# Last image of a two-layer kernel on one core: reciprocals spread by TensorE, the next layer's convolution inside the projection, depthwise taps shared with TensorE

## The chip, the cores and the metric

One core of one Trainium2 chip runs the whole kernel. The metric is the device time of one execution in microseconds (us). A core has five engines that run beside each other and wait for each other through semaphores: TensorE (PE, matrix products; PEld is its loading of weights), VectorE (DVE), ScalarE (ACT), GpSimd (POOL) and SyncE (SP, which here issues DMA transfers). PE writes only to the accumulation memory PSUM (eight banks of 128 partitions by 512 numbers of four bytes); the other data lies in the on-chip memory SBUF.

## The reference, cut to what matters

Eight images of 512 channels and 64 x 64 pixels pass through two layers, each added to its own input. All is in float32.

```python
# layer 0: attention with sampled keys and values
q = einsum('oc,bchw->bohw', w_q, gn(x))           # gn: mean and variance over 16 channels and all pixels
...                                               # 256 sampled positions per image and head -> k, v
attn = softmax(einsum('bhid,bhjd->bhij', q * scale, k))
out = einsum('bhij,bhjd->bhid', attn, v)
x = x + einsum('oc,bchw->bohw', w_out, out) + b_out

# layer 1: bottleneck
y = einsum('bchw,oc->bohw', gn(x), conv_w) + conv_b   # 512 -> 32 channels
z = depthwise_conv(y, dw_w) + dw_b                    # 3x3, stride 2: 64x64 -> 32x32
u = fc2(fc1(z))                                       # over the 1024 pixels, through 256
v = depthwise_deconv(u, de_w) + de_b                  # 3x3, 32x32 -> 64x64
x = x + einsum('bchw,oc->bohw', v, out_w) + out_b     # 32 -> 512 channels
```

## The kernel before, in words

An image lies in SBUF as nine slots of 512 pixels by four chunks of 128 channels; eight of them are pixel tiles, t = 0 to 7. Input, queries and outputs of tile t use different slots of the ring (`x_tile`, `q_tile`, `out_tile`), so that the output of tile t lies where the queries of tile t - 1 were. Two images are held at once (`region`, `spot`).

The order of all work is written out by hand in one loop over g (L1098), one step for each image, tile and pair of heads (256 steps), and LAG = 6 further steps which let the projections of the last tile finish. A step issues `weighted_values` (L591; the products of exponentials and values), in every second step `sum_exps` (L615; the denominators, by products with a selection matrix into the PSUM tile pn), then `logits` of the next step, and `project_out` (L661) for the step six earlier: eight products of 128 x 64 weights with 512 columns into one bank, then on DVE an addition of bias and residual (L674) and the tile's statistics (L677, kept in `st`). Beside this, a generator issues the work of layer 1 for the image before and the queries of the image after; for the last image there is none of the latter.

After the fourth pair of heads of a tile, `invert` (L634) takes the reciprocal of the denominators on DVE (rn, L638), and four small DMAs (L644) copy rows so that each group of 32 partitions has what it needs. `scale_two` (L647) then, two pairs of heads at a time, spreads a row over 32 partitions with a DVE shuffle (L651) and multiplies the attention output with it (L653). `load_residual` (L655) fetches the residual of tile t into its output slot, when the projection of the tile before no longer reads it as queries.

For the last image layer 1 runs alone, after the loop (`layer1_last`, L1157). `layer1` (L730) begins with the loads of the fc2 weights (L736) and `group_stats` (L164): aggregates per chunk on DVE (L169), a product with a 128 x 128 matrix that averages over groups of 16 channels (L173), variance on DVE (L177 to L179), a second such product (L182), and a power of -0.5 on POOL (L185). The convolution weights are scaled by the result (cw, L743). The convolution (py, L750) is 2 halves x 4 chunks x 4 blocks of rows, 32 products of 128 x 32 weights with 512 columns; ACT copies both halves to y (L762); the mean's part comes as 16 products with one column (pb, L768) and is added on DVE (L777). Three copies (L779) bring the last row of one block of rows to the next. The depthwise convolution is nine DVE instructions (L795, L797), each over 256 numbers with a column of weights; then a transpose (pz, L803), fc1 (ph L814, pht L828) and fc2 (pu, L848). `upsample` (L867) makes the transposed convolution of one half of the pixel rows and one parity a of rows, on DVE (L881, L883): three instructions for a = 0 and six for a = 1.

`project_last` (L949) then takes six banks at a time: output products of 32 x 128 weights (L893), and for each result either one addition on DVE (L980), or, for two of the eight tiles, an evacuation on ACT (L977) and an addition on POOL (L978). Each result goes out with its own DMA of 256 KB from SP (L983), 32 in all. Last, a check on the size of the logits (L1163 to L1178) decides on a second path, which these inputs don't take.

Of the kernel before, what the change touches and what calls it, by code (L numbers as in the profile page):

```python
# [49 lines left out]
def kernel(  # L50
# [610 lines left out]
    def project_out(b, t, oc, st):  # L661
# [3 lines left out]
        for hp in range(NCC):  # L665
            for r in (0, DH):
                nc.tensor.matmul(  # L667
                    pp[r : r + DH, :],
                    wout[:, hp, oc * P + r : oc * P + r + DH],
                    ao[:, hp, :],  # L670
                    start=(hp == 0),
                    stop=(hp == NCC - 1),
                )
        nc.vector.scalar_tensor_tensor(  # L674
# [53 lines left out]


    def layer1(b, st, project, place, v):  # L730
# [10 lines left out]
        gs = yield from group_stats(st, 1, b)  # L741
        cw = small.tile([P, NCC, CB], F32, tag="cw", name=f"cw_{b}")
        nc.vector.tensor_mul(cw, convw, gs[:, 1].unsqueeze(2).to_broadcast([P, NCC, CB]))  # L743
        yield None

        py = [ps_mm.tile([P, TP], F32, tag="mm", name=f"py_{b}_{h}") for h in range(2)]
        for h in range(2):
            for cc in range(NCC):
                for rb in range(4):
                    nc.tensor.matmul(  # L750
                        py[h][rb * CB : (rb + 1) * CB, :],
                        cw[:, cc, :],
                        out_tile(b, 2 * rb + h)[:, cc, :],
                        start=(cc == 0),
                        stop=(cc == NCC - 1),
                    )

        y = wflat[:, : (ROWS + 1) * (HW + 1)].rearrange("p (r c) -> p r c", c=HW + 1)
        nc.vector.memset(y[:, :, 0:1], 0.0)
        nc.vector.memset(y[0:CB, 0:1, :], 0.0)  # L760
        for h in range(2):
            nc.scalar.copy(  # L762
                y[:, 1 + 8 * h : 9 + 8 * h, 1:], py[h].rearrange("p (r c) -> p r c", c=HW)
            )
        pb = ps_mm.tile([P, TP], F32, tag="mm", name=f"pb_{b}")
        for cc in range(NCC):
            for rb in range(4):
                nc.tensor.matmul(  # L768
                    pb[rb * CB : (rb + 1) * CB, 0:1],
                    cw[:, cc, :],  # L770
                    gs[:, 0, cc : cc + 1],
                    start=(cc == 0),
                    stop=(cc == NCC - 1),
                )
        yb = small.tile([P, 1], F32, tag="yb", name=f"yb_{b}")
        nc.vector.tensor_sub(yb, col(V_CONVB), pb[:, 0:1])
        nc.vector.tensor_scalar_add(y[:, 1:, 1:], y[:, 1:, 1:], yb)  # L777
# [11 lines left out]
        z3 = z.rearrange("p (i j) -> p i j", j=32)  # L789
        for k in range(9):  # L790
# [3 lines left out]
            if k == 0:  # L794
# [89 lines left out]

        for h, a in ((0, 0), (0, 1), (1, 0)):
            upsample(h, a)
            yield None
# [100 lines left out]
    def layer1_last(b, st, other):  # L988
        return layer1(b, st, project_last(other), spot(other, 0), wbuf[:, 0:2, :])
# [69 lines left out]
    with tc.manual_schedule():  # L1059
# [38 lines left out]
        for g in range(len(names) + LAG):  # L1098
# [12 lines left out]
            summed = g % 2 == 0 and 0 <= g - 1 < len(names)  # L1111
            if g % 2 == 0:
                scale_two()
            if g < len(names):
                weighted_values(*names[g])
            if summed:
                sum_exps(*names[g - 1])
            if g < len(names):
                add_exps(*names[g])
# [24 lines left out]
            if 0 <= k < len(names) and k % NCC < 2:  # L1144
                load_residual(*names[k + k % NCC], 2)
# [11 lines left out]
        drain(layer1_last(B - 1, st1s.pop(B - 1), B - 2))  # L1157
# [118 lines left out]
```

## Time and profile before

The time before is 3290.07 us, the median of three runs (3289.28 to 3290.38).

| what | us |
|---|---|
| median of the runs | 3290.07 |
| the profiled execution | 3290.23 |
| its span, first to last instruction | 3288.5 |
| last loop product of attention values and projection pp(6,1) ends | 3193.1 |
| reciprocal of the last tile ends | 3197.8 |
| projections pp(6,2) and pp(6,3) end | 3201.1 |
| projection of the last tile, pp(7,0) to pp(7,3), ends | 3221.7 |
| convolution py ends | 3237.1 |
| depthwise result z complete | 3243.8 |
| fc2 (pu) ends; its bias added (u) | 3251.1; 3252.07 |
| first addition of an output block on DVE (L980) | 3258.2 |
| last store issued | 3282.4 |

pp(t,oc) is the projection of tile t to output chunk oc. Times from the start of the span are read from the chain of waits and from the timeline of the last 100 us, which list instructions by start and length. In the timeline a product of float32 shows as two records, and records of a column-tiled product overlap, so that the distance between starts, not the length of one, tells the rate. A name such as rn or pp is the program's name for a tile, and L638 is a line of the kernel. The granted clock (PEclk) is given as a share of full speed.

### The profile page before, as it was taken

The numbers are of one execution on the slowest core, as the hardware profiler recorded it, in microseconds if no ns is written. First come the engines' busy times: TensorE is split into PE (matmuls) and PEld (weight loads), VectorE is DVE, ScalarE is ACT, GpSimd is POOL, SyncE is SP. The second block draws the span as 40 slices with busy tenths as digits, with TensorE's granted clock in tenths as the row PEclk, the third lists the DMA queues.
The fourth block names the chain that finished last, engine by engine and source line by source line (L and its number), as shares of the span: only waits on it lengthen the run. The fifth ranks groups of instructions, "written<-read, shape, count | busy, mean of one in ns | idle before, by whom it ended". The sixth has DMA issues, their size and how long they took to land.

```text
span 3288.5 us, 46198 instructions
## 1 busy us (share of the span) xinstructions
PE 3207.7 (98%) x18196; PEld 1531.2 (47%) x18196; DVE 2330.8 (71%) x3786; ACT 1186.2 (36%) x1641; POOL 612.2 (19%) x576
## 2 busy tenths in 40 slices
PE   6999999999999999999999999999999999999996
PEld 5884223348332583326733276332853338433222
DVE  7884765787757777587765977668776687757564
ACT  2343333343333433344333443324433344333520
POOL 1130300130402304022030221303021040310201
PEclk9999999999999999999999999999999999999996
DMA  7232222672327623284333843248232482322713
GB/s 275 77 93 76 76 78 65 198 156 75 113 91 213 126 86 103 78 235 115 104 100 103 209 100 111 83 160 194 71 104 89 181 180 65 121 73 77 130 44 125
DMA packets 293874, 390.62 MB, mean 119 GB/s; under 512 B 18320, under 2 KB 157840, under 8 KB 293648
## 3 DMA queue, kind: packets, MB, share of 16 engines
q1 hardware_dynamic: 240368, 261.72, 24.4%
q0 software_dynamic: 53280, 125.86, 17.1%
q8 instruction: 145, 2.38, 0.3%
q14 instruction: 81, 0.66, 0.1%
HBM read 193.52 MB, written 192.94 MB: 118 GB/s over the span
## 4 chain that ended last, share of the span: by engine, by line
PE 94%; DVE 4%; issue 1%; ACT 0%; DMA 0%; SPq 0%; POOL 0%; ACTq 0%; DVEq 0%; POOLq 0%
PE pp L667 27%; PE pq L275 23%; PE ps L580 14%; PE pa L598 13%; PE pn L625 4%; PE pqt L324 4%; PE pk L533 2%; PE py L750 2%; PE pv L560 2%; PE po L893 2%; DVE rn L638 1%; PE po L424 0%; PE pu L848 0%; DVE st L201 0%; PE po_s L893 0%
## 5 line engine op out<-in xcount | busy, mean ns | idle before, releaser
L667 PE MATMUL pp<-image,wout 128*64 128x512 f32 x3584 | 821.3, 600 | 3.6 <-DVE image L653 3.4
L588 ACT ACTIVATE es<-ps 128x1024 f32<-128x1024 f32 x512 | 504.0, 1022 | 274.0 <-PE ps L580 211.1
L667 PEld LDWEIGHTS pp<-image,wout 128*64 128x64 f32 x3584 | 237.3, 137 | 549.5 <-issue 474.6
L598 PE MATMUL pa<-es,vt 128*64 128x512 f32 x2048 | 488.9, 598 | 1.7 <-ACT es L588 1.7
L275 PE MATMUL pq<-image,wbuf 128*128 128x256 f32 x2048 | 476.3, 381 | 3.3 <-DVE image L217 1.9
L519 POOL DMA_INDIRECT g<-qd,row x256 | 280.4, 1095 | 1056.2 <-DVE row L516 990.0
L580 PE MATMUL ps<-image,kt 64*64 64x512 f32 x3584 | 437.3, 602 | 0.3
L275 PEld LDWEIGHTS pq<-image,wbuf 128*128 128x128 f32 x2048 | 381.8, 191 | 56.0 <-issue 5.0
L674 DVE SCALAR_TENSOR_TENSOR image<-pp,vec,image 128x512 f32<-128x512 f32 x224 | 167.2, 746 | 337.8 <-PE pp L667 334.2
L605 ACT COPY image<-pa 128x512 f32<-128x512 f32 x224 | 131.9, 589 | 658.9 <-PE pa L598 650.5
L610 DVE TENSOR_TENSOR es<-es,es 128x1024 f32<-128x1024 f32 x256 | 310.9, 1215 | 71.4 <-PE pa L598 71.4
L598 PEld LDWEIGHTS pa<-es,vt 128*64 128x64 f32 x2048 | 137.3, 137 | 294.5 <-issue 274.1
L580 PEld LDWEIGHTS ps<-image,kt 64*64 64x64 f32 x3584 | 114.4, 132 | 307.4 <-issue 182.0
L638 DVE RECIPROCAL rn<-pn 128x512 f32<-128x512 f32 x64 | 214.6, 3353 | 7.7 <-PE pn L625 5.8
L334 ACT COPY qr<-pqt 128x512 f32<-128x512 f32 x224 | 131.0, 585 | 238.7 <-PE pqt L324 223.8
L185 POOL TENSOR_TENSOR gs<-ve,nhalf 128x4 f32<-128x4 f32 x16 | 16.6, 1040 | 1022.5 <-DVE ve L184 1022.5
L651 DVE STREAM_SHUFFLE rb<-rn 128x512 f32<-128x512 f32 x256 | 187.4, 732 | 0.1
L275 PE MATMUL pq<-es,es 128*128 128x256 f32 x768 | 181.5, 379 | 0.0
L945 POOL DMA_DIRECT2D out_dram<-part x126 | 138.1, 1324 | 153.9 <-ACT part L940 146.6
L201 DVE BATCH_NORM_STATS2 st<-image 128x6 f32<-128x512 f32 x256 | 159.2, 678 | 7.5 <-DMA image<-in_x_dram 7.4
L677 DVE BATCH_NORM_STATS2 st<-image 128x6 f32<-128x512 f32 x224 | 155.6, 695 | 7.7
L653 DVE TENSOR_TENSOR image<-image,rb 128x512 f32<-128x512 f32 x224 | 155.2, 693 | 7.8
(197 smaller groups left out, 3491.6 us busy)
## 6 DMA issues: line engine op xcount, KB each, us to landing
qd<-qr SPq DMA_DIRECT2D x256, 256.0 KB
image<-in_x_dram SPq DMA_DIRECT2D x112, 512.0 KB
out_dram<-image SPq DMA_DIRECT2D x49, 1024.0 KB
image<-in_x_dram POOLq DMA_DIRECT2D x48, 1024.0 KB
out_dram<-part POOLq DMA_DIRECT2D x126, 256.0 KB
image<-in_x_dram SPq DMA_DIRECT2D x16, 1024.0 KB
wbuf<-in_w_kvT_dram SPq DMA_DIRECT2D x14, 1024.0 KB
out_dram<-spare POOLq DMA_DIRECT2D x56, 256.0 KB
```

The costliest lines, as they stand in the source:

```text
L201: nc.vector.bn_stats(st[:, cc, t, :], x_tile(b, t)[:, cc, :])
L275: nc.tensor.matmul(bank[:, o * 2 * P : (o + 1) * 2 * P], w[:, k, o * P : (o + 1) * P], xh[:, k, :], start=(k == 0), stop=(k == 1),)
L519: nc.gpsimd.indirect_dma_start(held[-1][:, i, :, :].rearrange("p j d -> p (j d)"), None, qd[:, :], bass.IndirectOffsetOnAxis(ap=row[:, ky, ...
L580: nc.tensor.matmul(ps[k : k + DH, a, :], kt[r : r + DH, hp, kc * P + k : kc * P + k + DH], qt[r : r + DH, hp, :], start=True, stop=True,)
L588: nc.scalar.activation(e, ps, AF.Exp)
L598: nc.tensor.matmul(pa[a * DH : (a + 1) * DH, :], vt[:, kc, hd * DH : (hd + 1) * DH], es[kc][:, a, :], start=(kc == 0), stop=(kc == 1),)
L610: nc.vector.tensor_add(es[0], es[0], es[1])
L638: nc.vector.reciprocal(rn, denominators.pop((b, t)))
L651: nc.vector.stream_shuffle(rb, rn, [2 * (hp % 2) + hp // 2] * 32)
L667: nc.tensor.matmul(pp[r : r + DH, :], wout[:, hp, oc * P + r : oc * P + r + DH], ao[:, hp, :], start=(hp == 0), stop=(hp == NCC - 1),)
L674: nc.vector.scalar_tensor_tensor(xt[:, oc, :], pp, col(V_BOUT + oc), xt[:, oc, :], ALU.add, ALU.add)
L677: nc.vector.bn_stats(st[:, oc, t, :], xt[:, oc, :])
```

## The change

Only the end of the last image is touched. The loop now has 256 steps instead of 262, and what its last six did is written out after it:

- The denominators of the last tile are summed, and their reciprocal rn is taken. The four DMAs and the shuffles are gone for this tile. Instead eight products with a column of the identity matrix as broadcast weights spread the rows of rn over 64 partitions each, into four banks, and DVE multiplies the attention output by these, all four pairs of heads, ahead of the projection pp(6,3).
- ACT scales the identity matrix by ten columns of depthwise weights, which gives ten diagonal matrices, in the tiles that held exponentials.
- `last_tile` projects the four chunks of tile 7. After three of the four pairs of heads of chunk oc it issues the statistics of chunk oc - 1 (`mean`) and the scaling of the convolution weights of chunk oc - 2 (`scale`). The convolution follows by chunks, with the statistics of the last chunk among them, and the mean's part ahead of the last two chunks.
- The bias and the mean's part are added when py is copied from PSUM, one half on ACT, one on DVE.
- Taps 5 to 8 of the depthwise convolution are products with diagonal matrices, into a bank that DVE adds to its own sum of taps 0 to 4.
- In the transposed convolution, the odd rows (six taps for each half) are products with diagonal matrices, written to every second column of a bank, and ACT moves them out with the bias. The even rows stay on DVE. All of them are issued ahead of the output products.

Other images take the same instructions as before (`convolve` and `convolve_mean` are only moved out).

```diff
-    def project_out(b, t, oc, st):
+    def project_out(b, t, oc, st, between=None):
...
+            if between:
+                between(hp)
...
+    def last_tile(b, st):
...
+        def mean(cc):
+            c = slice(cc, cc + 1)
+            nc.vector.bn_aggr(mv[:, cc, :], st[:, cc].rearrange("p t s -> p (t s)"))
+            nc.tensor.matmul(gps[0][:, c], group, mv[:, cc, 0:1], start=True, stop=True)
+            nc.vector.tensor_copy(gs[:, 0, c], gps[0][:, c])
+            nc.vector.tensor_sub(dv[:, c], mv[:, cc, 0:1], gs[:, 0, c])
+            nc.vector.tensor_mul(dv[:, c], dv[:, c], dv[:, c])
+            nc.vector.tensor_add(dv[:, c], dv[:, c], mv[:, cc, 1:2])
+
+        def scale(cc):
+            c = slice(cc, cc + 1)
+            nc.tensor.matmul(gps[1][:, c], group, dv[:, c], start=True, stop=True)
+            nc.vector.tensor_scalar_add(ve[:, c], gps[1][:, c], EPS)
+            nc.gpsimd.tensor_tensor(gs[:, 1, c], ve[:, c], nhalf[:, c], ALU.pow)
+            nc.vector.tensor_scalar(cw[:, cc, :], convw[:, cc, :], gs[:, 1, c], None, ALU.mult)
+
+        def between(oc):
+            def step(hp):
+                if hp == 2 and oc >= 1:
+                    mean(oc - 1)
+                    if oc >= 2:
+                        scale(oc - 2)
+
+            return step
+
+        for oc in range(NCC):
+            project_out(b, t, oc, st, between(oc))
...
+        convolve(b, py[:, 0, :], cw, 0, 0)
+        scale(2)
+        convolve(b, py[:, 1, :], cw, 1, 0)
+        convolve(b, py[:, 0, :], cw, 0, 1)
+        mean(3)
+        convolve(b, py[:, 1, :], cw, 1, 1)
+        scale(3)
+        for cc in range(NCC - 1):
+            convolve_mean(pb, cw, gs, cc)
+        for h in range(2):
+            convolve(b, py[:, h, :], cw, h, 2)
+        convolve_mean(pb, cw, gs, 3)
+        for h in range(2):
+            convolve(b, py[:, h, :], cw, h, 3)
+        return (py[:, 0, :], py[:, 1, :]), pb
...
+            py, pb = conv()
+            nc.vector.tensor_sub(yb, col(V_CONVB), pb)
+            for h in range(2):
+                to, fr = y[:, 1 + 8 * h : 9 + 8 * h, 1:], py[h].rearrange("p (r c) -> p r c", c=HW)
+                if h:
+                    nc.vector.tensor_scalar_add(to, fr, yb)
+                else:
+                    nc.scalar.activation(to, fr, AF.Identity, bias=yb)
...
+            if diag and k > 4:
+                nc.tensor.matmul(pd, diag[V_DWW + k], yk, start=(k == 5), stop=(k == 8))
+                if k == 8:
+                    nc.vector.tensor_add(z, z, pd)
...
+            for h, tag in enumerate(("pa", "pn")):
+                upsample(h, 0)
+                pv = ps_a.tile([P, TP], F32, tag=tag, name=f"pv_{b}_{h}")[:, : 2 * P]
+                rows = pv.rearrange("p (r c) -> p r c", c=HW)
...
+                    for n, (k, dr, dc) in enumerate(taps):
+                        nc.tensor.matmul(
+                            rows[:, :, c::2],
+                            diag[V_DEW + k],
+                            u[:, 4 * h + dr : 4 * h + dr + 4, dc : dc + 32],
+                            start=(n == 0),
+                            stop=(n == len(taps) - 1),
+                        )
+                nc.scalar.activation(
+                    v[:, h, :].rearrange("p (r c) -> p r c", c=HW)[:, 1::2, :],
+                    rows,
+                    AF.Identity,
+                    bias=col(V_DEB),
+                )
...
-        for g in range(len(names) + LAG):
+        for g in range(len(names)):
...
-        drain(layer1_last(B - 1, st1s.pop(B - 1), B - 2))
+
+        b, t, st = B - 1, NT - 1, st1s.pop(B - 1)
+        sum_exps(*names[-1])
+        rn = small.tile([P, TP], F32, tag="rn", name="rn_last")
+        nc.vector.reciprocal(rn, denominators.pop((b, t)))
+
+        diag = {}
+        for i, w in enumerate([V_DWW + k for k in range(5, 9)] + [V_DEW + k for k in (0, 1, 2, 6, 7, 8)]):
+            diag[w] = es4[i // 8][:, i // 4 % 2, i % 4 * P : (i % 4 + 1) * P]
+            nc.scalar.activation(diag[w], ident, AF.Copy, scale=col(w))
+        project_out(b, t - 1, 2, st)
+        rb = [ps_s.tile([P, 2, TP], F32, tag="s", name=f"rb_last_{i}") for i in range(2)]
+        for hp in range(NCC):
+            for a in range(2):
+                row = CB * (2 * a + hp % 2) + hp // 2
+                nc.tensor.matmul(
+                    rb[hp // 2][a * DH : (a + 1) * DH, hp % 2, :],
+                    ident[:, row : row + 1].to_broadcast([P, DH]),
+                    rn,
+                    start=True,
+                    stop=True,
+                )
+        for hp in range(NCC):
+            ao = q_tile(b, t)[:, hp, :]
+            nc.vector.tensor_mul(ao, ao, rb[hp // 2][:, hp % 2, :])
+        project_out(b, t - 1, 3, st)
+        for oc in (0, 2):
+            load_residual(b, t, oc, 2)
+        drain(layer1_last(b, st, b - 1, lambda: last_tile(b, st), diag))
```

## The prediction

> **What bounds the kernel now.** The page first: it says that TensorE is the chain that ended last for 94% of the span, so a change of one image's ending can only win the stretch in which PE waits there.
>
> ```profile
> span 3288.5 us, 46198 instructions
> PE   6999999999999999999999999999999999999996
> PEclk9999999999999999999999999999999999999996
> PE 94%; DVE 4%; issue 1%; ACT 0%; DMA 0%; SPq 0%; POOL 0%; ACTq 0%; DVEq 0%; POOLq 0%
> ```
>
> Both PE and its granted clock are full until the last of the 40 slices (82 us each). The second view is the chain of waits in order of time over the last 100 us; columns are start, length, what.
>
> ```profile
> 3194.48 3.34 DVE rn L638
> ...
> 3199.71 1.69 DMA rn<-rn
> ...
> 3207.32 14.39 PE pp L667 x56
> ...
> 3226.52 1.04 POOL gs L185
> ...
> 3227.93 9.18 PE py L750 x64
> ...
> 3248.96 2.18 PE pu L848 x28
> ```
>
> From 3194 the chain leaves PE (reciprocal, a DMA of rows, shuffles and products on DVE), returns for the projection of the last tile (end 3221.7), leaves it for the statistics (six small steps), and then alternates up to the first output product. Third, windows of 1 us and 2 us (length, then busy time of PE, PEld, DVE, ACT, POOL with counts, then clock, DMA share, GB/s):
>
> ```profile
> 3204.00:3205.00 1.00, 0.67 (x4) 0.20 (x4) 1.00 (x2) 0.00 (x0) 0.00 (x0) 0.90 0.88 303
> 3205.00:3206.00 1.00, 1.00 (x4) 0.00 (x0) 0.97 (x4) 0.00 (x0) 0.00 (x0) 0.50 0.94 221
> 3211.00:3212.00 1.00, 1.00 (x4) 0.16 (x4) 0.92 (x2) 0.00 (x0) 0.00 (x0) 0.69 0.29 100
> 3246.00:3247.00 1.00, 1.00 (x12) 0.18 (x4) 0.00 (x0) 0.00 (x0) 0.00 (x0) 0.50 0.00 0
> 3267.00:3269.00 2.00, 2.00 (x9) 0.97 (x9) 1.83 (x6) 0.42 (x2) 1.27 (x1) 0.50 1.03 381
> 3281.00:3283.00 2.00, 0.00 (x0) 0.00 (x0) 0.00 (x0) 0.00 (x0) 0.00 (x0) 0.50 0.72 261
> ```
>
> Each idle stretch costs twice: the wait, and half a clock for the matmuls behind it. And from 3265 the DMA engines are full (381 GB/s) with the 32 stores of 256 KB: the ending is a fixed drain behind the first output block, so what the change wins is how much earlier that block comes. The timeline has the first L980 (output addition on DVE) at 3258.16.
>
> **What the Trainium skill says.** TensorE: Matmul & The Clock Gate, Part 1 (What's actually happening): the clock is halved or restored at the ends of free-running windows of about 3.4 us, by how busy PE was in one. The trace agrees: it falls near 3204.9, rises near 3211.7, falls near 3225.6, rises near 3232.1, falls near 3242.7, that is 2, 4, 2 and 3 such windows apart. A window with PE busy 1.42 of 3.4 us (3201.5 to 3204.9) ended in half clock, one with 1.73 (3235.6 to 3239.0) didn't. The same page (Architectural detail) calls VectorE's queue strict FIFO; the trace has nothing against it. PSUM — Partial Sum Buffer, Specifications (TRN2), says that any non-contiguous access slows matmuls significantly, without a figure; no matmul of the kernel before writes PSUM with a step, so nothing here shows it.
>
> **The change part by part.** Times are on the span of the profiled execution.
>
> *Reciprocals.* Gone: four DMAs of rows, four shuffles, and the wait between projections. The order on PE is now: denominators, pp(6,2), eight spreading products, pp(6,3), tile 7. pp(6,2) ends at 3197.5 as before (32 matmul records of two projections took 7.09 us, 3.55 each); rn is ready at 3197.85. The spread has the shape of a projection (eight products, 128x64 weights, 512 columns): 3.55 us, to 3201.4. DVE meanwhile does pp(6,2)'s addition and statistics (0.68 + 0.69, to 3199.2) and four multiplications; reading PSUM I take L674's 0.75 rather than L653's 0.69, so 3202.3. pp(6,3) hides them (to 3205.0). So tile 7 starts with no wait at 3205.0, against pieces from 3203.15 and mostly from 3207.3 at half clock. The residual loads still wait for pp(6,3), which reads the same buffer: before, they were issued at 3200.3 and the first 512 KB had moved by 3203.2; 2.9 us after 3205.0 is 3207.9, 0.6 us ahead of the first need (3208.55). The fc2 and fc1 loads behind them on SP come 5 us later and are needed at 3236 and after. The ten diagonals are some 3 us on ACT (ten of L822's size or less, 0.3 each), where nothing is until the image's evacuation: nothing.
>
> *Statistics inside the projection.* 4 x 3.55 = 14.2 us, plus five small products in PE's stream. L173's pair of records took 0.36 alone; I take that (bounds 0.12, the weights being prefetched, and 0.5): 1.8. Each waits for DVE, and DVE's queue has the POOL power (1.03) in it, with the weight scaling behind it. Per chunk DVE does copy, sub, mul, add, eps (1.0), waits 1.1, scales (0.2), adds (0.75), statistics (0.69), aggregate (0.3): 4.1, while PE takes 3.55 + 0.72; about level, and I add one stall of 0.2. Projection's end: 3205.0 + 14.2 + 1.8 + 0.2 = 3221.2, against 3221.7: the early start is spent on the insertions.
>
> *Convolution.* A chunk of four products is 8 of 64 records; at full clock the groups of four records took 0.43, so 0.86 a chunk. After 3221.2: two chunks and a small product and a third chunk to +2.95. DVE is late: its queue holds the scaling of chunk 1 (to +1.1), the last addition and statistics (+2.55), then scale(2) with its POOL wait (+4.0), and only then the last aggregate (+4.3). So mean(3) holds PE from +2.95 to +4.35. Then copy to add (+5.5), chunk to +5.55, scale(3) to +5.95, POOL to +7.2, weights at +7.4; PE in the meantime does means and chunks 4 to 6, ending at +8.1, and the last two at +9.8: 3231.0. Before: 3237.1. Gain 6.1.
>
> *Evacuation.* Before, a copy (0.6) and an addition over both halves (0.77): 1.41. Now bias in the evacuation, ACT and DVE each a half; DVE's 512 from PSUM about 0.7 (0.41 for L795's 256, plus 256 columns): +0.75. Gain 0.65. The three row copies (0.6) stay: y at 3232.4, against 3239.15.
>
> *Depthwise.* Before 0.42 + 8 x 0.52 = 4.6. Now DVE 0.42 + 4 x 0.52 = 2.5, with four diagonal products on PE beside it (two L275 records of 0.217 each, 1.75 in all), and an addition from PSUM (0.45): 3.0. Gain 1.6: z at 3235.4, against 3243.8.
>
> *fc1, fc2.* Nothing changed, but before they ran at half clock: pz 0.66, ph 1.97, pht 1.08, pu 2.18, 5.9 of 7.36 us. Now PE's gaps ahead are 1.4 and 1.4 us, not 6.6. If the clock holds, 2.95 less: u at 3235.4 + 4.4 + 0.95 = 3240.8, against 3252.07. Gain 11.3 in all; 8.3 if it doesn't hold.
>
> *Upsampling.* Before, the first output addition began 6.1 us after u, since DVE did all 18 taps. Now DVE does six (2.0), PE twelve. A 128-column product with new weights: L324's records stand 0.117 apart, two a tap: 0.235, 2.8 in all, at full clock. Output products stand behind both halves' taps on PE; + 0.6 for one, 0.05: first addition at u + 3.45. The taps write PSUM at step 2; if that doubles them, u + 6.25. Bounds 1 and 2 times; I take 1.5: u + 4.85, gain 1.25. The evacuation on ACT (0.4) is beside PE.
>
> *Drain.* 30.3 us from the first addition to the end. 8.39 MB at 381 GB/s is 22.0; the first 6 us before moved 232 to 380. With output products at full clock I take 0.5 off (0 to 1.5).
>
> Sum: 11.3 + 1.25 + 0.5 = 13.05, less 0.3 for semaphore hops in the new steps: 12.75. The profiled execution took 3290.23 (span 3288.5), which is 0.16 above the median 3290.07; 3290.23 - 12.75 = 3277.5.
>
> **The rivals.**
> A, as above, the clock full from 3211 on. For it: with the windows where they stand in the trace, the new stages fill them by half or more (pd 1.75 us in one, pz, ph and pht 2.0 in the next). Best, 1-times taps and 1.5 at the drain: 3290.23 - 15.2 = 3275.0; worst, 2-times taps, insertions of 0.5: 3280. Chance 0.62.
> B, the clock falls between the convolution and fc1. Worst window (from pd's end): pz and ph, 1.5 of 3.4 us, between the 1.42 that fell and the 1.73 that didn't, and the window's phase is free. Then fc1 and fc2 give nothing (8.3), taps take 5.6 at half clock and the first addition comes at u + 6.7 (loss 0.6): 8.3 - 0.6 + 0.5 - 0.3 = 7.9, 3282.3; from 3279 (falls late) to 3286. Chance 0.24.
> C, the insertions stall PE: residuals land 2 us later, or a POOL hop is 2 us, and mean() holds the projection in each of three chunks, some 5 us, partly recovered as DVE is then less behind: 3290.23 - 12.75 + 5 = 3282.5, and with a half clock inside 3285. Against it: the margins of 0.2 to 0.6 us above. Chance 0.08, half of it within 0.2%.
> D, slower: one mechanism, the step-2 writes to PSUM in the twelve taps. Each tap would have to be over 1.4 us (6 times 0.235) to eat the gain, and 2 us for 0.2% slower. At 10 times, 28.2 us, the first addition is at u + 28.9: 22.8 later than before, less 11.0 + 0.5: 3301.5. For it: the page's word and no row. Against: half the columns are merely skipped. Chance 0.06.
>
> **How the numbers follow.** A measurement of this kernel can tell about 0.2%, 6.6 us, from no change. Faster: A 0.62, three quarters of B 0.18, a quarter or so of C 0.02: 0.82. Within: the rest of B and C, 0.12. Slower: D, 0.06. The time is A's, 3277.5. The range, 3274 to 3284.5, is A's own with 1 us below it and most of B; left out are D, the bad part of C and the tail of B.
>
> **What would show it.** PE without a gap of over 0.5 us from 3197.9 to the projection's end near 3221; one wait of about 1.4 us behind the last aggregate; py's end near 3231; PEclk full at fc1; the first L980-type addition near 3245.7; 28 to 30 us of stores behind it. Wrong if the clock falls at fc1 (B), if a tap takes over 0.47 us, or if the projection's end is beyond 3224.

## The result, and the profile after

The changed kernel takes 3277.48 us (median of 6 runs, 3276.30 to 3278.57); beside it the kernel before took 3289.68 us (6 runs, 3288.31 to 3290.38). That is 12.2 us less, a ratio of 0.9964 (95% interval 0.9954 to 0.9974). In a later comparison it was 12.1 us less. The forecast was 3277.5. The profiled execution took 3278.57 us, the slowest of the six and 1.1 above the median, with a span of 3276.8.

The forecast total is right to a tenth of a microsecond, but it is not right by its own steps: the clock fell at fc1, which was rival B, and other steps made good for it. That they balance so closely is luck. The rest of this text is about that.

First the lines of the page that answer to those shown of the kernel before:

```profile
span 3276.8 us, 46318 instructions
PE   6999999999999999999999999999999999999997
PEclk9999999999999999999999999999999999999998
PE 94%; DVE 3%; issue 1%; ACT 0%; DMA 0%; SPq 0%; POOL 0%; ACTq 0%; DVEq 0%; POOLq 0%
```

Only the last slice differs: 7 for 6 in PE, 8 for 6 in its clock. At this scale nothing can be read of where the time went, so the chain of waits is next (start, length, what):

```profile
3194.33 3.35 DVE rn_last L1269
3197.72 3.65 PE rb_last L1280 x16
3201.37 9.44 PE pp L667 x44
...
3229.15 0.70 ACT wbuf L833
3229.88 0.77 DVE wbuf L831
...
3235.34 1.59 PE ph L896 x16
...
3238.79 2.18 PE pu L930 x28
...
3241.94 4.88 PE pv L980 x24
...
3247.92 7.40 DVE image L1090 x11
```

From the reciprocal's end to the end of py PE has no gap worth the name: the spread, then 44 records of projections in 9.44 us, which is pp(6,3), pp(7,0) and three quarters of pp(7,1). The chain leaves PE again only with the evacuation. Behind it the two rows to note are pu, 2.18 us as in the chain of the kernel before, and pv, the new taps, 4.88 us. Both are long because of the clock: the windows show its fall, and two experiments below show what full clock gives (columns as before: length, busy time of PE, PEld, DVE, ACT, POOL, then clock, DMA share, GB/s):

```profile
3202.00:3203.00 1.00, 1.00 (x8) 0.36 (x6) 0.71 (x2) 0.00 (x0) 0.00 (x0) 1.00 0.00 0
3233.00:3234.00 1.00, 0.00 (x0) 0.00 (x0) 0.86 (x3) 0.00 (x0) 0.00 (x0) 1.00 0.00 0
3235.00:3236.00 1.00, 0.67 (x12) 0.48 (x16) 0.28 (x1) 0.00 (x0) 0.00 (x0) 0.88 0.00 0
3236.00:3237.00 1.00, 0.90 (x12) 0.02 (x2) 0.00 (x0) 0.05 (x1) 0.00 (x0) 0.50 0.00 0
3246.00:3247.00 1.00, 1.00 (x11) 0.88 (x14) 0.00 (x0) 0.15 (x1) 0.00 (x0) 1.00 0.00 0
```

Where the kernel before had 0.50 at 3205 and 0.69 at 3211, the clock now is 1.00 right through the projection and the convolution. It falls once, near 3235.8 (0.88 over 3235 to 3236 means that it was halved for about the last quarter), and is back near 3246. The hole ahead of the fall is plain: in the microsecond from 3233 PE does nothing, because DVE still has taps of its own when the diagonal products are done.

The same stages side by side; the last two columns are this case's main reading. The forecast lengths are those of the prediction.

| stage | before, ends | after, ends | length after | length forecast |
|---|---|---|---|---|
| reciprocal of tile 7 | 3197.82 | 3197.68 | | |
| spread and pp(6,3); tile 7 starts | 3203.15, mostly 3207.3 | 3204.80 | 7.1 | 7.15 |
| projection of tile 7 | 3221.71 | 3220.38 | 15.6 | 16.2 |
| convolution py | 3237.11 | 3229.13 | 8.75 | 9.8 |
| y complete | 3239.14 | 3231.27 | 2.14 | 1.4 |
| z complete | 3243.8 | 3234.33 | 3.06 | 3.0 |
| u | 3252.07 | 3241.89 | 7.6 | 5.4 |
| first output addition | 3258.16 | 3247.92 | 6.0 | 4.85 |
| end of the span | 3288.5 | 3276.8 | 28.9 | 29.8 |

The gain, read down the two columns of ends, is 1.3 us at the projection's end, 8.0 at py's, 7.9 at y, 9.5 at z, 10.2 at u and at the first addition, and 11.7 at the end. So more than half of it, 6.7 us, comes between the end of the projection and the end of py, where the kernel before waited for the statistics and then convolved.

### The profile page after: what moved, and what is told of

Read it like the earlier page. It is cut to its first block, busy times and chain, and to the rows that moved or that the text cites. A ratio compares the mean times of both kernels' runs of the same rounds, so it can differ in the third digit from the quotient of the medians.

```text
span 3276.8 us, 46318 instructions
## 1 busy us (share of the span) xinstructions
PE 3209.6 (98%) x18256; PEld 1535.1 (47%) x18256; DVE 2325.3 (71%) x3781; ACT 1188.6 (36%) x1652; POOL 614.0 (19%) x579
## 4 chain that ended last, share of the span: by engine, by line
PE 94%; DVE 3%; issue 1%; ACT 0%; DMA 0%; SPq 0%; POOL 0%; ACTq 0%; DVEq 0%; POOLq 0%
PE pp L667 27%; PE pq L275 23%; PE ps L580 14%; PE pa L598 13%; PE pqt L324 4%; PE pn L625 4%; PE pk L533 2%; PE pv L560 2%; PE po L1003 2%; PE py L733 1%; DVE rn L638 1%; DVE image L1090 0%; PE po L424 0%; PE pu L930 0%; DVE st L201 0%
## 5 line engine op out<-in xcount | busy, mean ns | idle before, releaser
L598 PE MATMUL pa<-es,vt 128*64 128x512 f32 x2048 | 489.1, 598 | 1.7 <-ACT es L588 1.7
L598 PEld LDWEIGHTS pa<-es,vt 128*64 128x64 f32 x2048 | 137.4, 137 | 294.7 <-issue 274.8
L185 POOL TENSOR_TENSOR gs<-ve,nhalf 128x4 f32<-128x4 f32 x15 | 15.6, 1042 | 895.6 <-DVE ve L184 895.6
```

The costliest lines, as they stand in the source:

```text
L598: nc.tensor.matmul(pa[a * DH : (a + 1) * DH, :], vt[:, kc, hd * DH : (hd + 1) * DH], es[kc][:, a, :], start=(kc == 0), stop=(kc == 1),)
```

## The experiments

Times of a run are medians, with the kernel before run on the same chip beside them (3288.87 beside the first four, 3290.11 beside the next four, 3289.88 beside the last four). The span's first 3189 us shift by up to 2 us from one execution to the next, so stages are compared by their distance from the end of the last products of exponentials and values (the chain's last pa, L598, at 3189.45 after and 3189.61 before, where the main part ends). Each change below is made to the changed kernel.

**Part by part: the spread alone.** The last tile's spread stays; the projection is not interleaved, and layer 1 is the one of the kernel before.

```diff
-        diag = {}
...
-        drain(layer1_last(b, st, b - 1, lambda: last_tile(b, st), diag))
+        for oc in range(NCC):
+            project_out(b, t, oc, st)
+        drain(layer1_last(b, st, b - 1))
```

> The reciprocals' part alone; statistics, convolution, depthwise steps and upsampling as in the kernel before. Theory (each part is worth what its own stage shows, and the parts add): tile 7 starts without a wait at 3204.7 and, with nothing inserted, its projection ends 14.2 us later at 3218.9, 2.8 us ahead of the kernel before; from there the stages of the kernel before take their 36.5 us to the first output addition and 30.3 us to the end, span 3285.7. Rival (the early start was spent on the insertions alone, and elsewhere a later stage absorbs it): projection ends near 3219 but the span is within 1 us of 3288.5.

Measured: 3285.73 us (12 runs), 3.1 below the kernel before (ratio 0.9992, 0.9983 to 1.0001; the interval takes in no change, so the stages of the trace have to tell). The projection ends 29.12 us after the last pa, against 32.10 before and 30.93 in the changed kernel. Two terms follow. The spread by TensorE with its full clock is worth 3.0 us at the projection's end. And the five small products of the statistics cost the projection 30.93 - 29.12 = 1.8 us. Only 1.37 us of it is their own time; the rest is in their neighbours, as the changed kernel's chain shows:

```profile
3214.71 0.31 PE pa_last L766 x2
3215.03 0.22 PE pn_last L774 x2
3215.25 3.58 PE pp L667 x16
3218.83 0.31 PE pa_last L766 x2
3219.15 0.22 PE pn_last L774 x2
3219.37 1.01 PE pp L667 x4
3220.38 0.99 PE py_last L733 x8
```

No "issue" and no DVE stands between these lines: the statistics were never late. A run of 16 records between two insertions takes 3.58 us, while the 44 uncut ones took 9.44, that is 3.43 per 16.

**Without the spread.** The inverse, the four DMAs and the shuffles come back; all else is as changed.

```diff
-        rn = small.tile([P, TP], F32, tag="rn", name="rn_last")
-        nc.vector.reciprocal(rn, denominators.pop((b, t)))
+        invert(*names[-1])
...
         project_out(b, t - 1, 2, st)
-        rb = [ps_s.tile([P, 2, TP], F32, tag="s", name=f"rb_last_{i}") for i in range(2)]
...
+        scale_two()
         project_out(b, t - 1, 3, st)
...
+        scale_two()
```

> Row DMAs and shuffles as in the kernel before for the last tile; everything behind is that of the changed kernel. Theory: TensorE waits 2 us from 3201 and in pieces to 3207.3, falls to half clock, and the projection ends at 3221.7 plus the 1.4 us of inserted products, 3223.1, 2.7 us later than in the changed kernel; all later stages move with it, span 3279.5. Rival (in the projection with statistics inside it DVE sets the pace, so TensorE's wait is hidden): under 1 us later, span 3277.5 or less.

Measured: 3281.34 us (9 runs), 7.5 below the kernel before (0.9975, 0.9965 to 0.9985), so 4.7 of the changed kernel's 12.2 are lost. The projection ends 34.09 us after the last pa, 3.2 later than with the spread. The chain of this run shows how:

```profile
3194.87 3.34 DVE rn L638
...
3200.10 1.68 DMA rn<-rn
...
3208.51 0.69 DVE image L653
...
3209.26 5.27 PE pp L667 x16
```

From the reciprocal's end (3198.21) to the last multiplication (3209.20) DVE and the DMA hold the chain for 11 us, and the 16 records behind it take 5.27 us for 3.58 because the clock was halved in the gap. The remaining 1.5 us or so of the loss by medians is not settled by this run.

**Without the diagonal products**, depthwise taps and upsampling all on DVE again:

```diff
-        diag = {}
...
-        drain(layer1_last(b, st, b - 1, lambda: last_tile(b, st), diag))
+        drain(layer1_last(b, st, b - 1, lambda: last_tile(b, st)))
```

> Spread and chunked convolution kept, depthwise and transposed convolution all on DVE as before. Theory: y at 3231.3 as in the changed kernel, z 4.6 us later at 3235.9, fc1 and fc2 at half clock (8.3 us to u), first output addition at u + 6.1 = 3250.3, then 30.3 us of drain at half clock: span 3280.6, 3.8 us above the changed kernel. Rival (the diagonals give only the depthwise 1.6 us, and the drain is the stores' alone, 28.9 us): span 3279.2 or less.

Measured: 3280.81 us (10 runs), 8.1 below the kernel before (0.9975, 0.9965 to 0.9984). pz, which waits for z, starts 46.58 us after the last pa, against 44.93: the four depthwise diagonals are worth 1.65 us, as forecast (1.6). fc1 and fc2 ran at half clock here too, from 3232. By the medians all ten diagonals are worth 8.1 to 12.2, 4.1 us; z gives 1.65 of them and the first addition 2.3 in all (60.8 against 58.47). The rest is not settled by this run.

**Upsampling alone on DVE**, the four depthwise diagonals kept:

```diff
-        if diag:
+        if False:
```

> As the changed kernel, but the odd rows of the transposed convolution stay on DVE (depthwise diagonals kept). The taps on TensorE took as long as DVE did before, so the first output addition should come at u + 6.1, as in the changed kernel within 0.3 us (near 3248.0). Theory (the taps' only gain is that they bring TensorE back to full clock ahead of the output products): clock stays 0.50 in the output products, 30.3 us from the first addition to the end, span 3278.3. Rival (the drain is set by the stores and the clock does not matter there): 28.9 us, span 3276.9.

Measured: 3278.64 us (3277.09 to 3280.16, 8 runs), 10.2 below the kernel before (0.9968, 0.9957 to 0.9979): the taps on TensorE are worth about 2 us by the medians, though the ranges of the two kernels overlap. Its profiled execution, the lowest of its runs, is a lesson on its own. There ph took 1.12 us and pht 0.65, and only pu was at half clock (2.18): the same instructions up to u as in the changed kernel, but the clock fell later. So where the clock falls differs from one execution to the next, and a single profile of this kernel carries about 1 us of luck. The fall, at 3236.70, also came behind 3.41 us (from 3233.29) in which the profile has PE busy for 2.05: more than the 1.81 (3235.52 to 3238.93) that kept the clock in the kernel before.

The traces also show what this luck is. Within each trace the falls and rises of the clock are whole multiples of 3.41 us apart: 3235.77, 3246.01 and 3266.49 in the changed kernel (3 and 6 of them), 3204.80, 3211.63, 3225.28, 3232.11 and 3242.35 in the kernel before (2, 4, 2 and 3). But this grid lies elsewhere in the work from one execution to the next. Counted from the last pa, the clock fell after 46.32 us in the changed kernel. Here it was kept at the step after 45.02 us and fell at the next, after 48.43 us.

**One tile or two.** In the changed kernel y's two halves leave PSUM one after the other, not beside each other as forecast. The theory: both halves of py are one PSUM tile, so that the first reader waits for the last product of both, and the second reader for the first. Two tiles:

```diff
-        py = ps_s.tile([P, 2, TP], F32, tag="s", name=f"py_{nm}")
-        pb = ps_s.tile([P, 2, TP], F32, tag="s", name=f"pb_{nm}")[:, 0, 0:1]
+        py = [ps_s.tile([P, 2, TP], F32, tag="s", name=f"py_{nm}_{h}")[:, 0, :] for h in range(2)]
+        pb = ps_mm.tile([P, TP], F32, tag="mm", name=f"pb_{nm}")[:, 0:1]
```

> As the changed kernel, but the two halves of py are two PSUM tiles instead of two banks of one. In the changed kernel ACT's half began only when both halves were done, and DVE's half only when ACT's was done: 1.51 us from py's end. Theory (the waits belong to the shared tile): ACT begins one chunk earlier, DVE at py's end, the evacuation ends 0.8 us after py's end, 0.7 us saved. Rival (the waits belong to the shared destination y, or to the two readers of PSUM): DVE still waits for ACT, 0.1 us or less saved.

Measured: 3276.59 us (5 runs), 13.5 below the kernel before (0.9962, 0.9948 to 0.9977). The two instructions in the timeline of the changed kernel (start, length, engine, line; in brackets the idle time before and who ended it), where py ended at 3229.13:

```profile
3229.15 0.69 ACT L833 ACTIVATE wbuf<-py_last,yb 128x512 f32<-128x512 f32 x1 [36.15 <-PE py_last L733]
...
3229.88 0.75 DVE L831 TENSOR_SCALAR wbuf<-py_last,yb 128x512 f32<-128x512 f32 x1 [2.28 <-ACT wbuf L833]
```

and with two tiles, where py ended at 3228.19:

```profile
3227.35 0.69 ACT L833 ACTIVATE wbuf<-py_last,yb 128x512 f32<-128x512 f32 x1 [35.29 <-PE py_last L733]
...
3228.21 0.75 DVE L831 TENSOR_SCALAR wbuf<-py_last,yb 128x512 f32<-128x512 f32 x1 [1.56 <-PE py_last L733]
```

DVE's releaser changes from ACT to PE, and ACT now runs 0.84 us ahead of py's end, when its own half is done. From py to the start of pz it is 4.59 us for 5.25, 0.66 less. This is shown.

**A filled window.** The theory on fc1 and fc2: the clock is judged by how busy PE was in a window of about 3.4 us (the Trainium skill, TensorE: Matmul & The Clock Gate, What's actually happening; the grid of 3.41 us found above agrees), and the window that ends at the fall, 3232.36 to 3235.77, holds 1.33 us of PE. Three more products of the last depthwise diagonal, into a bank of PSUM that nobody reads, close the hole and change nothing else:

```diff
                 nc.tensor.matmul(pd, diag[V_DWW + k], yk, start=(k == 5), stop=(k == 8))
                 if k == 8:
+                    pf = ps_a.tile([P, TP], F32, tag="pa", name=f"fill_{b}")
+                    for _ in range(3):
+                        nc.tensor.matmul(pf[:, :NK], diag[V_DWW + k], yk, start=True, stop=True)
```

> As the changed kernel, with three more products of the last depthwise diagonal behind the four, into a bank that nobody reads, so that TensorE is busy for 1.3 us more while DVE finishes z. Theory (the clock falls at fc1 because a window of 3.4 us is less than half busy): PEclk stays full through fc1 and fc2, ph 1.1, pht 0.65, pu 1.1 us instead of 1.6, 1.1, 2.2, and the 24 tap records 0.117 us apart instead of 0.203; the first output addition is 4.1 us earlier, the median near 8.5 us... that is 16 us below the kernel before. Rival (the clock goes by something else, such as how many rows are driven, or the filler delays z's transpose): no gain, or a loss of up to 0.5 us.

Measured: 3274.60 us (3273.58 to 3277.72, 5 runs), 15.5 below the kernel before (0.9957, 0.9943 to 0.9972). The windows of this run where the changed kernel had 0.00 of PE and then the fall:

```profile
3233.00:3234.00 1.00, 0.84 (x5) 0.36 (x3) 0.80 (x2) 0.00 (x0) 0.00 (x0) 1.00 0.00 0
3235.00:3236.00 1.00, 0.99 (x16) 0.33 (x16) 0.00 (x0) 0.00 (x0) 0.00 (x0) 1.00 0.00 0
3236.00:3237.00 1.00, 0.52 (x4) 0.52 (x4) 0.00 (x0) 0.37 (x1) 0.00 (x0) 1.00 0.00 0
```

and its chain:

```profile
3234.92 1.11 PE ph L900 x16
...
3236.48 0.65 PE pht L914 x4
...
3237.46 1.22 PE pu L934 x28
...
3239.66 2.95 PE pv L984 x24
3242.60 1.08 PE po_s L1007 x8
```

The clock stays at 1.00. As it happens, the grid of its steps lies at the same place in the work in both traces, 46.32 and 46.33 us after the last pa, so the same window is compared, first without the three products and then with them:

```profile
3232.36:3235.77 3.41, 1.33 (x12) 0.51 (x15) 2.21 (x5) 0.00 (x0) 0.00 (x0) 1.00 0.00 0
```

```profile
3231.97:3235.38 3.41, 2.73 (x19) 1.63 (x21) 2.19 (x5) 0.00 (x0) 0.00 (x0) 1.00 0.00 0
```

ph, pht and pu together take 2.98 us for 4.85, the taps 2.95 for 4.88, and the first addition comes 54.67 us after the last pa instead of 58.47. The two differences, 1.87 and 1.93, make up these 3.8 us. Work that computes nothing made the kernel some 3 us faster: that fc1 and fc2 are long because of the clock, and that the clock falls for want of work on PE in the hole, is shown. How that work is counted is another question, to which the last runs return.

**The step in PSUM.** The same with the taps written side by side, and ACT putting the columns in order as it reads:

```diff
-                rows = pv.rearrange("p (r c) -> p r c", c=HW)
+                rows = pv.rearrange("p (c r k) -> p c r k", c=2, k=32)
...
-                            rows[:, :, c::2],
+                            rows[:, c],
```

> As the one with the filler, and the taps write PSUM without a step; ACT puts the columns in place when it reads. Theory (writes at step 2 cost nothing here, since the taps are paced by loading 128 x 128 weights): the tap records keep their distance within 3 per cent, time within 0.3 us of the one with the filler; ACT's evacuation may take 0.1 us more. Rival (step 2 doubles a tap): 24 records in half the time, 1.4 to 2.8 us saved.

Measured: 3274.25 us (4 runs), 15.9 below the kernel before (0.9956, 0.9939 to 0.9972). The line of its chain:

```profile
3239.32 2.94 PE pv L984 x24
```

24 records in 2.94 us beside 2.95 with the step: the step costs nothing here. The taps' 4.88 us in the changed kernel were the clock, and the mechanism of rival D isn't there. The Trainium skill (PSUM — Partial Sum Buffer, Specifications (TRN2)) warns of non-contiguous access in general; for these writes of 128 columns the measurement decides otherwise.

**Products between the taps.** In the changed kernel the first output products stand behind the taps of both halves on PE, but need only the first half. Here the taps of the second half come after the first six products:

```diff
-            for h, tag in enumerate(("pa", "pn")):
-                upsample(h, 0)
+            def odd_rows(h):
...
+            for h in range(2):
+                upsample(h, 0)
+            odd_rows(0)
+            yield from project(b, v, [lambda: odd_rows(1), lambda: None])
...
                         done.append((2 * rb + h, oc, po))
+                if rest:
+                    rest.pop()()
                 for t, oc, po in done:
```

> As the changed kernel, but the first six output products are issued between the taps of the first half and those of the second. Theory (the output products only wait behind the second half's 12 tap records on TensorE): the first output addition comes 12 x 0.203 = 2.4 us earlier, at u + 3.6, and the end follows: 2.4 us saved. Rival (the second group of output products now waits behind the taps and the stores run dry in between): 1 us saved or less.

Measured: 3282.79 us (13 runs), 7.3 below the kernel before (0.9978, 0.9970 to 0.9987): 5 us worse than the changed kernel. The first addition did come early, 4.8 us after u. ACT and DVE in the timeline show what is late behind it:

```profile
3248.79 0.47 ACT L986 ACTIVATE wbuf<-pv,vec 128x256 f32<-128x256 f32 x1 [3.61 <-PE pv L979]
3249.16 1.38 ACT L1092 ACTIVATE image<-po_s,vec 128x512 f32<-128x512 f32 x2
```

```profile
3246.40 1.41 DVE L1095 SCALAR_TENSOR_TENSOR image<-po_s,vec,image 128x512 f32<-128x512 f32 x2 [2.85 <-PE po_s L1006]
3249.87 0.75 DVE L1095 SCALAR_TENSOR_TENSOR image<-po_s,vec,image 128x512 f32<-128x512 f32 x1 [2.06 <-ACT image L1092]
```

ACT is at the evacuation of the second half, which waits 3.61 us for taps that now stand behind six products; ACT's evacuations for the first group (L1092) are queued behind it, and DVE's third addition waits 2.06 us for them. The DMA engines moved 262 GB/s from 3248 to 3250 and nothing from 3250 to 3252, while all but the first few stores were still to come. The clock then fell too, from 3251.66 to the end. This execution, 3280.14 us, is among the fastest of the 13, so its trace shows less than the loss by the medians. The next run puts the second evacuation on ACT behind the additions of the first group, and nothing else:

```diff
-                if rest:
-                    rest.pop()()
+                evacuate = rest.pop()() if rest else None
                 for t, oc, po in done:
...
+                if evacuate:
+                    evacuate()
                 yield None
```

> As the version that interleaves the output products with the taps, but ACT's evacuation of the second half is issued behind the additions of the first group. Theory (that version lost because ACT, in order, held back the first group's two blocks until the second half's taps were done, and the stores ran dry for 2 us): the first group's additions run through, the DMA engines stay full, and the time is 0.5 to 1.5 us below the changed kernel. Rival (it lost because the second group's products wait for the taps on TensorE): still slower than the changed kernel by 3 us or more.

Measured: 3277.28 us (3274.07 to 3281.67, 5 runs), 12.6 below the kernel before (0.9964, 0.9949 to 0.9978). The 5 us are gone, and in the profile the clock stays full up to 3265. The order on ACT is shown as the cause; how much of the loss was the wait and how much the clock that fell behind it is not separated:

```profile
3246.15 0.69 ACT L1091 ACTIVATE image<-po_s,vec 128x512 f32<-128x512 f32 x1 [1.29 <-PE po_s L1006]
3248.48 0.47 ACT L986 ACTIVATE wbuf<-pv,vec 128x256 f32<-128x256 f32 x1 [1.64 <-PE pv L979]
```

The gain over the changed kernel, run beside it on the same chip, is 0.5 us by the medians, within the spread of both; it isn't shown.

**The changed kernel again**, with nothing edited, as the measure for the last group of runs:

> The changed kernel itself, beside the others of this set on one chip. Expected 12.2 us below the kernel before, as in its first comparison, with profile stages within 0.2 us of those of its first profile up to z; behind z the stages depend on where the clock's window ends, 0 to 2 us.

Measured: 3277.77 us (3276.68 to 3278.94, 5 runs), 12.1 below the kernel before (0.9963, 0.9949 to 0.9977). The clock fell at about 3236.3; ph took 1.34 us for 1.59, pht and pu 1.08 and 2.17. Counted from the last pa, its stages up to z and its first addition stand within 0.1 us of those of the first profile; u comes 0.25 us earlier, and the taps take 5.12 us. Of the five traces of kernels that are alike up to u, the clock fell in ph or just ahead of it in four and later in one (upsampling on DVE): the fall at fc1 is the usual course and not an accident of one execution.

**Together.** Two tiles with the filling products:

> Two PSUM tiles for py, and the filler. Theory (the two are independent): 0.9 and 3.6 us together, 16.7 us below the kernel before. Rival (with y earlier the window of the clock moves and the filler's gain is lost): 13 to 14 us below.

Measured: 3275.61 us (3272.51 to 3276.43, 4 runs), 14.3 below the kernel before (0.9954, 0.9938 to 0.9971), where the sum of the two would give 16.7. In its profile fc1 and fc2 were at full clock (pu 1.22), but the clock fell at about 3240.5, in the taps. The window ahead of that fall, 3237.08 to 3240.49, holds none of the filling products, but 2.04 us of PE by the profile, in pht, pu and the first taps. So filling one hole keeps the clock for the window that holds it and no further, and PE's busy time alone, as the profile counts it, doesn't tell where the clock falls: with 2.04 it fell here and with 2.05 in the run with the upsampling on DVE, with 1.81 it was kept in the kernel before. There, two windows that the output products filled without a break did not even bring a halved clock back; it rose only behind a third, at 3273.07:

```profile
3262.83:3269.65 6.82, 6.82 (x24) 3.21 (x23) 6.30 (x13) 2.04 (x3) 3.49 (x3) 0.50 0.91 341
```

These windows hold products with few rows or columns of weights (32 columns in pu, 32 rows in the output products). Whether these count for less was not tried and stays open; the products of py, which were in the windows kept with 1.81, have 32 columns too. With the products between the taps, in the good order on ACT, added to this:

> Two PSUM tiles, filler, and the output products between the taps with ACT's second evacuation behind the first group. Theory: at full clock the second half's 12 tap records are 1.4 us, of which 0.5 goes to waiting for ACT's first evacuation: 0.9 us below the version without the interleaving, some 17.6 us below the kernel before. Rival (the stores are full already and TensorE's order no longer matters): within 0.3 us of it.

Measured: 3274.32 us (3272.93 to 3276.10, 4 runs), 15.6 below the kernel before (0.9955, 0.9939 to 0.9972). Its span of 3271.2 is the shortest of all, but by the medians it is not told from the filling alone. Its clock stayed full through the taps and fell at 3248.27, among the output products, behind a window with 2.81 us of PE. The kernels with filling products beat both kernels of this case; the simplest of them, with the three products alone, is 3 us below the changed one.

## Why the prediction was right, point by point

*The reciprocals: right.* The spread took 3.65 us (forecast 3.55), tile 7 started at 3204.80 (3205.0) with no wait, and DVE's multiplications were hidden by pp(6,3). The residuals, which come later now, held nobody: they were issued from 3203.1, and DVE's first addition of tile 7 began at 3208.29, with the end of pp(7,0).

*Statistics inside the projection: right, cheaper by 0.6.* 1.8 us for the insertions, against 1.8 and a stall of 0.2 that did not come; the projections took 3.43 us each and not 3.55, which is 0.5 over four. Rival C, insertions that stall PE, is out.

*Convolution: the mechanism right, one wait not there.* The forecast held PE 1.4 us at mean(3), because it gave the power on POOL 1.03 us, the size of the row of the kernel before. On one column it is shorter (timeline of the changed kernel):

```profile
3216.02 0.57 POOL L776 TENSOR_TENSOR gs_last<-ve_last,nhalf 128x1 f32<-128x1 f32 x1 [116.04 <-DVE ve_last L775]
```

With DVE's queue that much less behind, the product of mean(3) started 0.03 us after the one before it (3223.54 to 3223.57). The chunks cost 0.92 us each rather than 0.86 (7.36 us for the eight in the chain), which gives 0.5 back: 8.75 against 9.8.

*Evacuation: wrong by 0.7.* "ACT and DVE each a half" was priced as parallel. With one PSUM tile it was serial, 0.70 and 0.77 us one behind the other; two tiles took 0.66 of it away.

*Depthwise: right*, 3.06 us against 3.0.

*fc1 and fc2: wrong, the step that failed.* "If the clock holds, 2.95 less": it didn't hold, and by the prediction's own sign ("Wrong if the clock falls at fc1") the mechanism was wrong here, though the total was not. The forecast held the clock "with the windows where they stand in the trace", pd in one, pz, ph and pht in the next. But the grid is not fixed to the work: in the changed kernel a window ended inside pd, at 3232.36, and the next held only the last of pd, pz and the first part of ph, 1.33 us. Its own rival B named the worst window, with 1.5 of 3.4 us, and the two known cases around it. Read at the clock's own steps, these are 1.32 us, which fell (3201.39 to 3204.80), and 1.81, which didn't; the 1.42 and 1.73 of the prediction were read 0.1 us beside them. The window came out next to the one that fell; it held the same in the repetition (1.33) and with two tiles (1.32). As other runs fell with more, the two cases are not bounds that can be relied on.

u was 7.6 us after z and not 5.4. With the hole filled it was 5.7. So the length taken for full clock was nearly right, and the state was wrong: pz, ph, pht and pu took 3.43 us at full clock for 5.89 at half, 2.46 less where the forecast halved them. The longest gap in which nothing at all ran on PE was about 1.6 us. The Trainium skill (TensorE: Matmul & The Clock Gate, Why this matters for your kernels) advises against idle gaps of over about 3 us; here gaps of half that length, with short products around them, were enough.

*Taps: short by 1.15, and both terms wrong.* The forecast took one and a half times 2.8 us for the step in PSUM. The step cost nothing, and the clock, halved for all but the last 0.8 us of the taps, cost a factor of 1.65 (4.88 against 2.95 us), so that the first addition came 6.0 us after u instead of 4.85. With the clock held it was 4.1.

*Drain: 0.9 better than forecast, the cause shown only in part.* At full clock the first stores kept the DMA engines fed. Windows from 4 to 8 us behind the first addition, of the kernel before and of the changed kernel (the last number is GB/s):

```profile
3262.16:3264.16 2.00, 2.00 (x8) 0.51 (x4) 1.69 (x3) 0.96 (x2) 1.27 (x1) 0.50 0.89 339
3264.16:3266.16 2.00, 2.00 (x11) 1.10 (x8) 1.80 (x4) 0.00 (x0) 1.27 (x1) 0.50 0.77 286
```

```profile
3251.92:3253.92 2.00, 1.81 (x9) 0.60 (x10) 2.00 (x4) 0.63 (x1) 1.94 (x2) 1.00 1.00 380
3253.92:3255.92 2.00, 1.80 (x12) 0.59 (x6) 1.92 (x8) 0.69 (x1) 0.58 (x1) 1.00 1.02 384
```

The missing 41 and 94 GB/s over 2 us each are 270 KB, or 0.7 us at 380 GB/s. The kernel before took 30.3 us for the drain, the changed one 28.9. But the kernel without diagonals also drained at half clock, with nearly the same rates in these windows (329 and 294), and took 29.2, only 0.3 more than the changed one. So the clock explains a part of the 1.4 us at most, and the rest stays open.

The balance, measured less forecast: start of tile 7 -0.2, projection -0.6, convolution -1.05, y +0.75, z +0.05, u +2.2, first addition +1.15, drain -0.95, and less the 0.3 that the forecast allowed for hops, as what they took is already in these. That is +1.05 for the span, and 3278.57 less 3277.5 is 1.07; the median then lies 1.1 below that execution. Rival B was given 3282.3 and its clock came, but about 1.5 us of its price did not (pz and the first part of ph still had full clock, and its taps at half clock were set at 5.6 us and took 4.88), and the cheaper convolution and drain were not in its sum. The total is right because errors of up to 2.2 us in both directions cancel, and that is luck.

## What to carry to other kernels

When work is moved off TensorE or cut short on it, price what follows a hole of 1.6 us among short products at half clock, full clock being the lucky case, and try a few idle products in the hole before a cleverer schedule. Give two results that two engines read their own PSUM tiles. On an engine that works in order, an evacuation that has to wait belongs behind the ones that are ready, however early its line was written.

## What the runs showed that was not expected

The power on GpSimd took 0.57 us on 128 x 1 numbers and 1.04 on 128 x 4. A product of 128 x 128 weights of float32 with 128 columns, written with a step of 2, took 2.95 us for 24 records (0.123 each) at full clock and 4.88 us (0.203 each) with the clock halved for all but the last 0.8 us. A run of 16 projection records between two small products took 0.15 us more than 16 uncut ones, beyond the products' own time. The moment of the clock's fall wandered by 2.6 us between executions of kernels that are alike up to it (45.8 to 48.4 us after the last pa), and the times of such a kernel spread over 2 to 3 us (3276.3 to 3278.6, and 3277.1 to 3280.2 with the upsampling on DVE), so that a gain of 0.5 us, as of the products between the taps, can't be told in five runs.
